# Sums within PSUM in a feed-forward layer: shared partial sums copied bank to bank, and seven products for the first output block

## The chip, the cores and the metric

The kernel runs on one core of a Trainium2 chip. The metric is the device time of one execution in microseconds (us); less is better. The engines are TensorE (PE in the profile; PEld is its loading of weights), VectorE (DVE), ScalarE (ACT), GpSimd (POOL) and SyncE (SP), which issues most transfers between HBM and the core's memory, SBUF. Matmuls write into PSUM: eight banks of 128 x 512 fp32.

## The reference

One transformer layer on 16 sequences of 256 rows with 512 values each: cross-attention with 16 heads, then a feed-forward part. All of it is fp32.

```python
x = x + xattn(layernorm(x), ctx, mask, mask, Wq, bq, Wk, bk, Wv, bv)
# feed-forward: the weights are given as indices into a table of 16 values
def ghost_linear(x, idx, lut):
    return einsum('bsh,oh->bso', x, lut[idx])
y = layernorm(x)
gate = ghost_linear(y, gate_idx, lut)      # 512 -> 1376
up   = ghost_linear(y, up_idx, lut)        # 512 -> 1376
h    = silu(gate) * up
x    = x + ghost_linear(h, down_idx, lut)  # 1376 -> 512
```

The 16 x 256 rows of attention's output are 32 tiles of 128 rows. In the kernel they are taken as 8 blocks (`nblocks`) of 512.

## The kernel before, in words

The instructions of every engine stand in the order in which the program writes them (`manual_schedule`); the framework adds the waits. Attention takes the first 980 us and is not touched by the change, except that its pool of two double PSUM banks, `ps_a`, stays open afterwards. A second pool, `ps_b`, has four single banks. While attention runs, VectorE also looks up the weights: the indices become table values through bit tests and predicated copies (`look_up`). What is not looked up by then is done in the feed-forward part.

**Gate and up.** The index tiles become the weights `wg`, `wu` (512 x 1376 each, in four slices of 128) and later `wd` (1376 x 512, in 11 slices, the last of 96 rows). `gate_up(n, 0)` (L920) takes the first 128 hidden values of blocks n = 0 to 3 in the plain way: 2 x 4 products into a double bank of `ps_a`, Silu on ScalarE, the product with `up` on VectorE. All the rest goes in *units* (`unit`, L937): a unit takes one column `o` of 128 hidden values and one pair `p` of two blocks, and computes gate and up for both, a 2 x 2 by 2 x 2 block product, with seven half-size products instead of eight (Winograd's form of Strassen). Operands that are sums or differences of weights are in `sw` and, in place, in `wu` (`combine_w`); those of activations are in `xe` and, in place, in the turned activations `xT` (`combine_x`). A unit's seven products each take one bank of `ps_b`: two slices, which the trace shows as four matmul instructions of 512 columns. Seven additions on VectorE (L951) join them, ScalarE copies the first product and does two Silus, GpSimd does two multiplications (L974, L980), and the results `ha` and `hb`, tiles of 128 x 512, are stored to HBM (`store_h`, `hds`). There are 42 units, in the order written in `order`.

Between the additions of a unit, `fill(ns)` (L909) issues VectorE work from a list, `todo`: the lookups that are left and the sums of weights. A budget `room` in estimated ns rations it. `hooks` are three places in each unit at which the rows of the blocks 4 to 7 are loaded, normalized and turned (`turn_blocks`; the transposes go to a bank of `ps_a`).

**Down.** After the units, `load_h(1)` and `load_h(2)` load two blocks of hidden values from HBM (block 0 was loaded during pair 3, into tiles that had become free). The tiles of the new pool `hp` take memory that the units' pools (`sw`, `ht`) held until `first.close()`. Then VectorE makes the operands `t2`, `t4` from `wd` and `combine_h(1)` those of block 1. Block 0 goes the plain way: `down(0)` (L1129) has four row tiles, each of 11 slices of `wd` into one bank, 88 matmul instructions of 512 columns, and one addition of the residual rows `x2t`, which `load_x2` fetches. Blocks 1 to 7 go through `down7(n, t)` (L1143), two calls a block, of seven products each (1, 2, 6, 7, 5, 4, 3 in this order, 256 columns wide, five slices each and one more for the 96 rows in 2, 5, 4 and 3), joined by ten additions on VectorE. The residual rows are loaded at the top of the call and enter with the second addition, `add(p1, p1, xrs[0][:, lo])`. Between the two calls `combine_h(n + 1)` prepares the next block, and after them `load_h(n + 2)` follows.

Of the kernel before, what the change touches and what calls it, by code (L numbers as in the profile page):

```python
# [9 lines left out]
F32 = mybir.dt.float32  # L10
# [9 lines left out]
def kernel(  # L20
# [62 lines left out]
    ps_a = ctx.enter_context(tc.tile_pool(name="ps_a", bufs=2, space=PSUM))  # L83
# [99 lines left out]
    x3pool = []  # L183
# [20 lines left out]
    def turn2(k):  # L204
        n, t = divmod(k, 4)
        if t == 0:
            pool = xpool if n % 4 < FIRST else x3pool[0]
            xTs[n] = pool.tile([P, NH, 4 * P], F32, tag="xT", name=f"xT_{n}")
        if n < FIRST:
            pt = ps_b.tile([P, 512], F32, tag="b", name=f"pt_{k}")  # L210
        else:
            pt = ps_a.tile([P, 2, 512], F32, tag="a", name=f"pt_{k}")[:, 0, :]
        xn = xns.pop(k)
        for h in range(NH):
            nc.tensor.transpose(pt[:, h * P : (h + 1) * P], xn[:, h * P : (h + 1) * P], ident)  # L215
        nc.scalar.copy(xTs[n][:, :, t * P : (t + 1) * P], pt.rearrange("p (h r) -> p h r", r=P))


    with ExitStack() as att:
        ac = att.enter_context(tc.tile_pool(name="att_const", bufs=1))  # L220
# [584 lines left out]
    with ExitStack() as ffn:  # L805
        wd_pool = ffn.enter_context(tc.tile_pool(name="wd", bufs=1))
        xep = ffn.enter_context(tc.tile_pool(name="xe", bufs=2))
        x3pool.append(ffn.enter_context(tc.tile_pool(name="xT3", bufs=1)))
        first = ffn.enter_context(ExitStack())
        sp = first.enter_context(tc.tile_pool(name="ffns", bufs=1))  # L810
        lp = first.enter_context(tc.tile_pool(name="lookup2", bufs=1))
# [51 lines left out]
        def lookups():  # L863

            left = list(pieces_left())
            ids = {}

            def load(j):
                if j < len(left):
                    rows, n = left[j][1].shape  # L870
                    ids[j] = lp.tile([P, T], I32, tag="idx", name=f"idx_l{j}", bufs=2)[:rows, :n]
                    nc.sync.dma_start(ids[j], left[j][1])

            def each():
                for j, (to, of) in enumerate(left):
                    rows, n = of.shape
                    ops = look_up(
                        lambda tag: lp.tile([P, T], I32, tag=tag, name=f"{tag}_l{j}")[:rows, :n],
                        to, ids.pop(j),
                    )  # L880
# [39 lines left out]
        def gate_up(n, o):  # L920
# [3 lines left out]
            ps = ps_a.tile([P, 2, 512], F32, tag="a", name=f"pgu_{n}_{o}")  # L924
            for i, w in enumerate((wg, wu)):
                for h in range(NH):
                    nc.tensor.matmul(  # L927
                        ps[:rows, i, :], w[:, h, at], xTs[n][:, h, :],
# [3 lines left out]
            nc.scalar.activation(sg[:rows], ps[:rows, 0, :], AF.Silu)  # L932
            ht = f1.tile([P, 4 * P], F32, tag="ht", name=f"ht_{n}_{o}")
            v.tensor_tensor(ht[:rows], sg[:rows], ps[:rows, 1, :], ALU.mult)
            store_h(n, o, ht, rows)

        def unit(p, o, hooks):  # L937

# [5 lines left out]
            def product(i, a, b):  # L944
                ps = ps_b.tile([P, 512], F32, tag="b", name=f"p{i}_{p}_{o}")[:rows]
                for h in range(2):
                    nc.tensor.matmul(ps, a[:, h, at], b[:, h, :], start=h == 0, stop=h == 1)  # L947
                return ps

            def add(to, ps, other):  # L950
                v.tensor_tensor(to, ps, other, ALU.add)  # L951

            p1 = rpool.tile([P, 4 * P], F32, tag="us1", name=f"p1_{p}_{o}", bufs=1)[:rows]
            nc.scalar.copy(p1, product(1, a11, b11))
            w = rpool.tile([P, 4 * P], F32, tag="us0", name=f"w_{p}_{o}", bufs=5)[:rows]
            add(w, product(6, sw[:, 1], xe[:, 1]), p1)
            hooks[0]()
            fill(1000)
            sg = rpool.tile([P, 4 * P], F32, tag="rb", name=f"sg_{p}_{o}", bufs=1)[:rows]
            add(sg, product(2, a12, b21), p1)  # L960
            nc.scalar.activation(sg, sg, AF.Silu)  # L961
            fill(1000)
            r = rpool.tile([P, 4 * P], F32, tag="us0", name=f"r_{p}_{o}", bufs=5)[:rows]
            add(r, product(7, a21, xe[:, 0]), w)
            hooks[1]()
            fill(1000)
            p5 = product(5, sw[:, 0], t1)
            add(w, p5, w)
            hb = f1.tile([P, 4 * P], F32, tag="ht", name=f"hb_{p}_{o}")[:rows]
            add(hb, p5, r)  # L970
            fill(350)
            ha = f1.tile([P, 4 * P], F32, tag="ht", name=f"ha_{p}_{o}")[:rows]
            add(ha, product(4, a22, xe[:, 2]), r)
            nc.gpsimd.tensor_tensor(ha, ha, sg, ALU.mult)  # L974
            store_h(2 * p, o, ha, rows)
            hooks[2]()
            fill(1000)
            add(w, product(3, sw[:, 2], b22), w)
# [3 lines left out]
            fill(2500)  # L982
# [69 lines left out]
        hs = {}  # L1052
        for i, (p, o) in enumerate(order):
            if p < 2 and o in (5, 8):
                while o not in ready:
                    next(todo)[1]()
            if (p, o) == (3, 2):

                parts = [xpool.tile([P, NH, 4 * P], F32, tag="xT", name=f"h0_{j}") for j in range(2)]
                parts.append(xep.tile([P, 3, 2, 4 * P], F32, tag="xe", name="h0_2")  # L1060
                             .rearrange("p a b t -> p (a b) t"))
                hs[0] = []
                for j, part in enumerate(parts):
                    for q in range(4 * j, min(4 * j + 4, NO)):
                        hs[0].append(part[:, q - 4 * j, :])
                for j, part in enumerate(parts[:2]):
                    nc.sync.dma_start(part, hds[0][4 * j : 4 * j + 4].rearrange("o p t -> p o t"))
                nc.sync.dma_start(parts[2][:, 0:2], hds[0][8:10].rearrange("o p t -> p o t"))
                rows = rows_of(NO - 1)
                nc.sync.dma_start(parts[2][:rows, 2, :], hds[0][NO - 1, :rows, :])  # L1070
            unit(p, o, [lambda i=i, j=j: run(hooks.pop((i, j), ())) for j in range(3)])
        for _, op in todo:
            op()
        first.close()
        hp = ffn.enter_context(tc.tile_pool(name="ffnh", bufs=2))

        def load_h(n):
            h = hp.tile([P, NO, 4 * P], F32, tag="h", name=f"h_{n}")
            rows = rows_of(NO - 1)
            nc.sync.dma_start(h[:, 0 : NO - 1, :], hds[n][0 : NO - 1].rearrange("o p t -> p o t"))  # L1080
            nc.sync.dma_start(h[:rows, NO - 1, :], hds[n][NO - 1, :rows, :])
            return h

# [6 lines left out]
        wl, wh, wz = wd[:, 0:HO], wd[:, HO : 2 * HO], wd[:last_rows, NO - 1]  # L1090

# [6 lines left out]
        hn = {1: load_h(1), 2: load_h(2)}  # L1098
        t2 = part_of(x3pool[0].tile([P, NH, 4 * P], F32, tag="xT", name="t2"), 0)
        t4 = hp.tile([P, HO, 2 * P], F32, tag="t4", name="t4", bufs=1)  # L1100
        s1s = [None, part_of(xpool.tile([P, NH, 4 * P], F32, tag="xT", name="s1_1"), 0)]
        se = [None, xep.tile([P, 3, 2, 4 * P], F32, tag="xe", name="se_1")]
        v.tensor_tensor(t2, wh[:, :, hi], wl[:, :, hi], ALU.subtract)
        v.tensor_tensor(t2, t2, wl[:, :, lo], ALU.add)
        v.tensor_tensor(t4, wh[:, :, lo], t2, ALU.subtract)

        def combine_h(n):

            h = hn[n]
            s1, e = s1s[n % 2], se[n % 2]  # L1110
            s2, s4 = part_of(e, 0), part_of(e, 1)
            d = e.rearrange("p a b t -> p (a b t)")[:last_rows, 2 * HO * 2 * P : (2 * HO + 1) * 2 * P]
            a11, a21 = h[:, 0:HO, lo], h[:, 0:HO, hi]
            a12, a22 = h[:, HO : 2 * HO, lo], h[:, HO : 2 * HO, hi]
            yield v.tensor_tensor(s1, a21, a22, ALU.add)
            yield v.tensor_tensor(s2, s1, a11, ALU.subtract)
            yield v.tensor_tensor(a21, a11, a21, ALU.subtract)
            yield v.tensor_tensor(s4, a12, s2, ALU.subtract)
            z = h[:last_rows, NO - 1]
            yield v.tensor_tensor(d, z[:, lo], z[:, hi], ALU.subtract)  # L1120
# [5 lines left out]
        def new_ob(i, name):  # L1126
            return rpool.tile([P, T], F32, tag=("rb", "xr")[i], name=name, bufs=1)

        def down(n):  # L1129
            xrs = [load_x2(4 * n + t) for t in range(4)]  # L1130
            for t in range(4):
                po = ps_b.tile([P, 512], F32, tag="b", name=f"po_{n}_{t}")
                for o in range(NO):
                    rows = rows_of(o)
                    nc.tensor.matmul(  # L1135
                        po, hs[n][o][:rows, t * P : (t + 1) * P], wd[:rows, o, :],
                        start=(o == 0), stop=(o == NO - 1),
                    )
                ob = new_ob(t % 2, f"ob_{n}_{t}")
                v.tensor_tensor(ob, po, xrs[t], ALU.add)  # L1140
                store_rows(4 * n + t, ob)

        def down7(n, t):  # L1143

            h = hn[n]
# [105 lines left out]
```

## Time and profile before

| | |
|---|---|
| time, median of 3 runs | 1805.18 us (1804.65 to 1806.34) |
| the profiled execution | 1806.96 us, its span 1805.2 us |
| busy share of the span | PE 99%, DVE 81%, ACT 44%, POOL 28% |
| attention | up to 980 us |
| four `gate_up` calls | 980 to 1011.7 us |
| 42 units | 1011.7 to 1525.4 us |
| `down(0)` | 1525.4 to 1563.2 us |
| 14 calls of `down7` | 1563.2 us to the end |

The profile is of one execution. Its tables give, for each engine, how long it was busy, what ended the idle time before its instructions (the releaser), and the chain of work that ended last, followed back from the last instruction. Line numbers (L947) are those of the kernel before. A group such as `p<-xe,wu` is named by the tiles that an instruction writes and reads. A transfer's row on SP's queue shows when SP issued it, not when it landed. The trace's ends of matmuls are modelled, so the distance between the starts of two products is the better measure of their cost.

### The profile page before, as it was taken

What the parts mean: (1) busy time and instruction counts of PE and PEld (TensorE: products, weight loads), DVE (VectorE), ACT (ScalarE), POOL (GpSimd) and SP (SyncE); (2) the same over time, 40 slices, a digit from 0 to 9 for tenths busy, and PEclk for the clock granted to TensorE, in tenths of its full rate; (3) what the DMA queues carried; (4) which work ended last, traced back from release to release, by engine and by line L of the source; (5) the groups of instructions that cost most, each with busy time, mean ns of one, the idle gap of its engine ahead of it and who ended that gap; (6) DMA issues with size and microseconds to landing.
All of it is one profiled execution on the core that took longest, in us unless ns stands there. A gap on an engine that the chain in (4) does not pass through costs nothing.

```text
span 1805.2 us, 28544 instructions
## 1 busy us (share of the span) xinstructions
PE 1785.9 (99%) x10914; PEld 822.4 (46%) x10914; DVE 1460.8 (81%) x2030; ACT 798.1 (44%) x1523; POOL 500.3 (28%) x467
## 2 busy tenths in 40 slices
PE   8999999999999999999999999999999999999999
PEld 4333333333333333333343444444444444688887
DVE  6898899999898999998987799998989995353352
ACT  1777777777777777777775111112121111000000
POOL 4334333434343433344332122221222222000000
PEclk9999999999999999999999999999999999999999
DMA  6445544333433344444433111222121311444441
GB/s 184 126 149 149 146 124 123 124 105 111 128 122 116 95 128 140 145 115 141 122 102 92 59 53 66 80 87 92 68 99 49 115 45 59 169 133 135 170 133 58
DMA packets 118824, 201.07 MB, mean 111 GB/s; under 512 B 21780, under 2 KB 23960, under 8 KB 118688
## 3 DMA queue, kind: packets, MB, share of 16 engines
q1 hardware_dynamic: 114416, 196.21, 34.2%
q0 software_dynamic: 3168, 1.86, 0.5%
q8 instruction: 86, 1.41, 0.3%
q10 hardware_dynamic: 1104, 1.19, 0.2%
q14 instruction: 50, 0.41, 0.1%
HBM read 135.83 MB, written 58.10 MB: 107 GB/s over the span
## 4 chain that ended last, share of the span: by engine, by line
PE 91%; DVE 4%; DMA 2%; ACT 1%; issue 0%; SPq 0%; POOL 0%; ACTq 0%; POOLq 0%; DVEq 0%
PE p L947 27%; PE pa L490 15%; PE pv L537 12%; PE pb L498 11%; PE q L1154 10%; PE pv L413 3%; PE pq L413 3%; PE pk L413 3%; PE po L1135 2%; DVE nm L506 1%; DMA x2t<-x 1%; PE q L1159 1%; PE pgu L927 1%; PE pt L215 1%; PE pv L516 1%; DVE chosen L161 0%
## 5 line engine op out<-in xcount | busy, mean ns | idle before, releaser
L506 DVE TENSOR_REDUCE nm<-pa 128x2 f32<-128x1024 f32 x512 | 602.3, 1218 | 84.4 <-PE pb L498 79.3
L510 ACT ACTIVATE pt<-pb 128x512 f32<-128x512 f32 x1024 | 530.4, 602 | 105.5 <-PE pb L498 104.2
L490 PE MATMUL pa<-kp,qp 32*128 32x512 f32 x2048 | 513.9, 616 | 7.3 <-DVE nm L506 3.8
L498 PE MATMUL pb<-qp,kp 32*128 32x512 f32 x2048 | 517.5, 617 | 0.0
L490 PEld LDWEIGHTS pa<-kp,qp 32*128 32x128 f32 x2048 | 177.0, 184 | 201.0 <-DVE nm L506 151.7
L537 PE MATMUL pv<-pt,va 128*32 128x512 f32 x2048 | 246.2, 598 | 0.0
L498 PEld LDWEIGHTS pb<-qp,kp 32*128 32x128 f32 x2048 | 209.6, 183 | 74.0 <-issue 42.0
L947 PE MATMUL p<-xe,wu 128*128 128x512 f32 (+1 forms) x336 | 158.0, 592 | 0.3 <-DVE w L951 0.3
L947 PE MATMUL p<-xT,sw 128*128 128x512 f32 (+1 forms) x336 | 157.9, 592 | 0.0
L947 PE MATMUL p<-xT,wg 128*128 128x512 f32 (+1 forms) x336 | 157.9, 592 | 0.0
L974 POOL TENSOR_TENSOR ha<-ha,sg 128x512 f32<-128x512 f32 (+1 forms) x42 | 61.1, 1456 | 343.2 <-DVE ha L951 332.7
L979 ACT ACTIVATE w<-w 128x512 f32<-128x512 f32 (+1 forms) x42 | 26.5, 630 | 250.6 <-DVE w L951 250.6
L537 PEld LDWEIGHTS pv<-pt,va 128*32 128x32 f32 x2048 | 53.4, 109 | 173.1 <-ACT pt L510 97.1
L521 POOL DMA_DIRECT2D qp<-mx x64 | 38.4, 601 | 310.9 <-DVE mx L520 290.5
L1170 ACT COPY q<-q 128x256 f32<-128x256 f32 x14 | 5.2, 373 | 255.1 <-PE q L1154 255.1
L542 ACT COPY us<-pv 128x512 f32<-128x512 f32 x128 | 75.0, 586 | 94.7 <-PE pv L537 94.7
L947 PEld LDWEIGHTS p<-xe,wu 128*128 128x128 f32 (+1 forms) x336 | 62.9, 187 | 81.9 <-issue 72.0
L947 PEld LDWEIGHTS p<-xT,wg 128*128 128x128 f32 (+1 forms) x336 | 62.6, 187 | 78.8 <-issue 75.6
L947 PEld LDWEIGHTS p<-xT,sw 128*128 128x128 f32 (+1 forms) x336 | 62.1, 187 | 75.9 <-issue 74.7
L961 ACT ACTIVATE sg<-sg 128x512 f32<-128x512 f32 (+1 forms) x42 | 26.5, 630 | 143.4 <-DVE sg L951 143.4
L549 POOL TENSOR_TENSOR us<-us,us 128x512 f32<-128x512 f32 x64 | 82.4, 1287 | 15.1 <-ACT us L542 15.0
L429 POOL TENSOR_TENSOR natk<-natk,mb 128x512 f32<-128x512 f32 x31 | 41.0, 1322 | 147.1 <-ACT natk L426 141.8
(208 smaller groups left out, 2385.5 us busy)
## 6 DMA issues: line engine op xcount, KB each, us to landing
x2t<-x SPq DMA_DIRECT2D x96, 256.0 KB
h<-h SPq DMA_DIRECT2D x7, 2560.0 KB
kp<-kd SPq DMA_DIRECT2D x62, 256.0 KB
qp<-qd SPq DMA_DIRECT2D x62, 256.0 KB
h<-ha SPq DMA_DIRECT2D x38, 256.0 KB
h<-hb SPq DMA_DIRECT2D x38, 256.0 KB
rb<-rd SPq DMA_DIRECT2D x32, 256.0 KB
xr<-in_x_dram SPq DMA_DIRECT2D x32, 256.0 KB
```

Source lines behind the costliest of these rows:

```text
L413: nc.tensor.matmul(ps[32 * j : 32 * j + 32], weights(o, slice(first + 32 * j, first + 32 * j + 32)), moving(o), start=(o == 0), stop=(o == ...
L429: nc.gpsimd.tensor_tensor(t, t, mb, ALU.mult)
L490: nc.tensor.matmul(pa[:, jj, :], qps[ua % 4][at, ca * P : (ca + 1) * P], kps[ua % 4][at, :], start=True, stop=True,)
L498: nc.tensor.matmul(pb, kps[ub % 4][at, cb * P : (cb + 1) * P], qps[ub % 4][at, :], start=True, stop=True,)
L506: nc.vector.tensor_reduce(nms[ua][:, 2 * half : 2 * half + 2, ca], pa, AX.X, ALU.max, negate=True)
L510: nc.scalar.activation(pts[sb][:, j, :], pb, AF.Exp)
L537: nc.tensor.matmul(ps[32 * j : 32 * j + 32, :], va[:, at : at + 32], pt[:, j, :], start=(i == 0), stop=(i == 1),)
L542: nc.scalar.copy(us[u, half], ps)
L549: nc.gpsimd.tensor_tensor(a, a, b, ALU.add)
L947: nc.tensor.matmul(ps, a[:, h, at], b[:, h, :], start=h == 0, stop=h == 1)
L974: nc.gpsimd.tensor_tensor(ha, ha, sg, ALU.mult)
L1154: nc.tensor.matmul(ps, a[:, o, first_t], b[:, o, :], start=o == 0, stop=o == HO - 1 and not more,)
```

## The change

It has three parts.

1. *Units.* PSUM is divided anew: `ps_a` closes with attention, and `ps_f` opens, with three banks `ae` and one bank `pt` for the transposes. In a unit the first product goes to a bank `pa`, and ScalarE copies it to a bank `pb` of `ps_b`. Product 6 is accumulated onto `pa`, which ScalarE copies to `pc`; product 7 is accumulated onto `pa` again, which is copied to `pd`. Product 2 goes onto `pb`, 3 onto `pc`, 4 onto `pd`: their matmuls add to what ScalarE put there. Product 5 (`pe`) is copied to SBUF (`p5`), and VectorE adds it to `pa` and to `pc`. The multiplication for `ha` moves from GpSimd to VectorE and is held until the next unit has issued its first product (`held`). The arguments of `fill` become larger.
2. *Lookups and gate/up of column 0.* The lookup tiles become parts of one tile, `look`, that stays until the end; `gate_up` takes two single banks of `ps_b`.
3. *Block 0.* It goes through `down7` too. Its operands are put into the memory of `wg` and `wu`. `before_down` gives the nine steps that VectorE needs for them; two are issued in the last unit, three before `down7(0, 0)`, and four inside it, one behind each of its first four additions. The blocks' hidden values are loaded in a low part (five slices) and a high part (six); the low part of block 1 is loaded into `look` at unit (3, 5), after the rest of `todo`.

```diff
-    ps_a = ctx.enter_context(tc.tile_pool(name="ps_a", bufs=2, space=PSUM))
...
     with ExitStack() as att:
+        ps_a = att.enter_context(tc.tile_pool(name="ps_a", bufs=2, space=PSUM))
...
+        ps_f = ffn.enter_context(tc.tile_pool(name="ps_f", bufs=3, space=PSUM))
...
         def unit(p, o, hooks):
...
+            def product(ps, a, b, onto=True):
+                for h in range(2):
+                    nc.tensor.matmul(
+                        ps, a[:, h, at], b[:, h, :], start=h == 0 and not onto, stop=h == 1,
+                        skip_group_check=onto,
+                    )
+
+            def copied(name, ps):
+                to = bank(name)
+                nc.scalar.copy(to, ps)
+                return to
+
+            pa = bank("pa", ps_f, "ae")
+            product(pa, a11, b11, onto=False)
+            pb = copied("pb", pa)
+            fill(600)
+            if held:
+                held.pop()()
+            pe = bank("pe", ps_f, "ae")
+            product(pe, sw[:, 0], t1, onto=False)
+            p5 = rpool.tile([P, 4 * P], F32, tag="us1", name=f"p5_{p}_{o}", bufs=1)[:rows]
+            nc.scalar.copy(p5, pe)
+            fill(2000)
+            product(pa, sw[:, 1], xe[:, 1])
+            pc = copied("pc", pa)
+            hooks[0]()
+            fill(2000)
+            product(pb, a12, b21)
+            sg = rpool.tile([P, 4 * P], F32, tag="rb", name=f"sg_{p}_{o}", bufs=1)[:rows]
+            nc.scalar.activation(sg, pb, AF.Silu)
+            fill(2000)
+            product(pa, a21, xe[:, 0])
+            pd = copied("pd", pa)
+            hooks[1]()
+            hb = f1.tile([P, 4 * P], F32, tag="ht", name=f"hb_{p}_{o}")[:rows]
+            v.tensor_tensor(hb, pa, p5, ALU.add)
+            fill(1000)
+            product(pc, sw[:, 2], b22)
             w = rpool.tile([P, 4 * P], F32, tag="us0", name=f"w_{p}_{o}", bufs=5)[:rows]
...
+            v.tensor_tensor(w, pc, p5, ALU.add)
             nc.scalar.activation(w, w, AF.Silu)
             nc.gpsimd.tensor_tensor(hb, hb, w, ALU.mult)
             store_h(2 * p + 1, o, hb, rows)
-            fill(2500)
+            product(pd, a22, xe[:, 2])
+            hooks[2]()
+            fill(1700)
+
+            def hold():
+                ha = f1.tile([P, 4 * P], F32, tag="ht", name=f"ha_{p}_{o}")[:rows]
+                v.tensor_tensor(ha, pd, sg, ALU.mult)
+                store_h(2 * p, o, ha, rows)
+
+            held.append(hold)
...
+        def before_down():
+
+            c = combine_h(0)
+            yield next(c)
+            yield next(c)
+            yield v.tensor_tensor(t2, wh[:, :, hi], wl[:, :, hi], ALU.subtract)
+            yield v.tensor_tensor(t2, t2, wl[:, :, lo], ALU.add)
+            yield next(c)
+            yield v.tensor_tensor(t3, wh[:, :, hi], wl[:, :, hi], ALU.subtract)
+            yield v.tensor_tensor(wl[:, :, hi], wl[:, :, hi], wl[:, :, lo], ALU.subtract)
+            yield v.tensor_tensor(t4, wh[:, :, lo], t2, ALU.subtract)
+            yield from c
...
+            if (p, o) == (3, 5):
+                for _, op in todo:
+                    op()
+                h_parts[1] = [(0, look[:, 0:HO])]
+                load_part(1, *h_parts[1][0])
+            if (p, o) == order[-1]:
+                pre = before_down()
+                hooks[i, 1].append(lambda: next(pre))
+                hooks[i, 2].append(lambda: next(pre))
             unit(p, o, [lambda i=i, j=j: run(hooks.pop((i, j), ())) for j in range(3)])
...
         def load_h(n):
...
+            low = look[:, 0:HO] if n % 2 else hp.tile([P, HO, 4 * P], F32, tag="hl", name=f"hl_{n}", bufs=1)
+            h_parts[n] = [(0, low)]
+            load_part(n, 0, low)
+            load_high(n)
...
+        def down7(n, t, pre=iter(())):
...
             xrs = [load_x2(4 * n + t), load_x2(4 * n + t + 2)]
...
             def add(to, ps, other):
                 v.tensor_tensor(to, ps, other, ALU.add)
+                next(pre, None)
...
-        for _ in combine_h(1):
-            pass
-        down(0)
...
+        load_high(1)
+        load_h(2)
+        for _ in range(3):
+            next(pre)
+        down7(0, 0, pre)
+        new_e(1)
+        for n in range(nblocks):
+            if n:
+                down7(n, 0)
             if n + 1 < nblocks:
                 for _ in combine_h(n + 1):
                     pass
             down7(n, 1)
```

## The prediction, made before the changed kernel was run

> **What bounds the kernel now.** I read the page first: part 1 for the busy shares, part 4 for the chain that ended last. Then I asked for TensorE's waits from 975 us on, where the changed code begins, and for the timelines of one unit and of the passage from the units to the down products.
>
> ```profile
> PE 1785.9 (99%) x10914; PEld 822.4 (46%) x10914; DVE 1460.8 (81%) x2030; ACT 798.1 (44%) x1523; POOL 500.3 (28%) x467
> PE 91%; DVE 4%; DMA 2%; ACT 1%; issue 0%; SPq 0%; POOL 0%; ACTq 0%; POOLq 0%; DVEq 0%
> ```
>
> TensorE (PE) is busy for 1785.9 of 1805.2 us and carries 91% of the chain. VectorE (DVE) at 81%, ScalarE (ACT) at 44% and GpSimd (POOL) at 28% only matter where they make PE wait. How often they do, in the stretch that the change touches:
>
> ```profile
> PE pt L215 <- ACT xT L216: 1.5, 2, 0.8
> PE q L1154 <- DVE ob L1166: 1.3, 2, 0.9
> PE p L947 <- DVE hb L951: 0.8, 1, 0.8
> PE pgu L927 <- POOL rb L592: 0.7, 1, 0.7
> PE p L947 <- DVE w L951: 0.3, 1, 0.3
> ```
>
> The columns are us in total, times, longest. The 42 units (L947) lose 0.8 + 0.3 = 1.1 us altogether, so relieving VectorE there can give back no more than that. What is left to gain is PE work itself. From the chain in order of time and the timeline:
>
> ```profile
> 1525.40 37.78 PE po L1135 x88
> 1563.18 4.32 PE q L1154 x20
> 1580.03 4.32 PE q L1154 x20
> ...
> 1501.20 1.88 PE L947 MATMUL p<-xT,wg 128*128 128x512 f32 x4
> 1502.92 1.88 PE L947 MATMUL p<-xe,sw 128*128 128x512 f32 x4
> 1503.17 0.59 ACT L954 COPY p<-p 128x512 f32<-128x512 f32 x1 [0.42 <-PE p L947]
> 1504.64 1.88 PE L947 MATMUL p<-xT,wg 128*128 128x512 f32 x4
> ```
>
> The first two columns are start and us. Down products of block 0 take 37.78 us in the plain form; one call of `down7` takes 1580.03 - 1563.18 = 16.85 us. In a unit the starts of successive products lie 1502.92 - 1501.20 = 1.72 us apart. The copy of a product starts 0.25 us after the product's last issue slot (1503.17 against 1502.92) and takes 0.59 us.
>
> **The change, part by part.** The sum is made against the profiled execution's span, 1805.2 us; that execution took 1806.96 us with what lies around the span, while the three timed runs have the median 1805.18. So differences in the span are added to 1805.18. A measurement of this kernel tells about 0.2%, 3.6 us, from no change.
>
> *Units.* Each keeps 7 products of 4 matmul instructions, 7 x 1.72 = 12.0 us of PE, times 42 as before: nothing there. VectorE loses four of seven additions of 0.68 us (42 x 4 x 0.68 = 114 us), GpSimd one of two multiplications of 1.47 us (about 61 us); ScalarE gains three copies of about 0.6 us (75 us), being busy 1.8 of 12 us in a unit now. None of this is on the path; its worth is at most the 1.1 us of waits. In exchange PE gets three new waits per unit: product 6 onto the sum that `pb` was copied from, 7 after the copy `pc`, 4 after the copy `pd`. Each time one other product (5, 2, 3) of 1.72 us lies between the product that is copied and the waiting one, and the copy needs 0.25 + 0.59 = 0.84 us of it, which leaves 0.88 us. No row shows ScalarE writing PSUM; its rows beside this, 0.373 us (128x256 copy) and 0.63 us (Silu), bound it, and I take 0.59: the cover holds up to 1.47 us. In front of these copies on ScalarE's queue stand the Silu of `w`, which waits for VectorE's addition, and the transposes' copies; with the units' VectorE order that addition may be about 2.9 us late before `pb` is, and one `combine_x` (4 x 1.23 us) fits into its idle time. I take back half of the 1.1 us: -0.6, with 0 to -1.1 for the range. The `fill` budgets rise from 6.85 to 9.3 us a unit, so the lookups, whose last instruction now ends at 1495.7, two and a half units before the end, are done near unit 30 of 42; the forced rest at (3, 5) finds nothing, and the load of block 1's low part that follows it has ten units to land. The store of `ha` moves into the next unit, on SP behind whatever hook 2 loads: nobody waits for it but the third `ht` buffer, a unit later, so 0.
>
> *Gate and up of column 0.* Two single banks for one double one; the four calls stay 32 + 16 + 16 instructions on PE. The banks they inherit from the scores were emptied by 980.05 (copy of the last `pv`), and the one needed then is used from 982.8. The 1.5 us of the transposes stay: one `pt` bank now, and the second transpose already waits for the first one's copy. 0.
>
> *Block 0 by seven products.* 37.78 us become 2 x 16.85 = 33.70: -4.08 us, if nothing waits. But the plain form needed nothing from VectorE. The new one needs `s1`, `s2`, `t2`, `t3`, the turned halves of `h` and `wl`, `t4`, `s4`, in VectorE instructions of 1.48 us (rows of L1103, L1115 to L1118 and L1195), nine steps, of which four come inside `down7`, each behind one of its additions. Call T0 the time of its first product (1525.2 now). Unhindered, product 6 starts at T0 + 4.75, product 7 at T0 + 6.9, product 5 at T0 + 9.1. On VectorE two steps run in the last unit, the held product of `ha` comes at T0 + 1.6 and three steps follow until about T0 + 6.2. The addition behind product 6 ends at T0 + 7.5, `t3` at T0 + 9.1: product 7 starts 2.2 us late.
>
> *The wait that I expect to decide.* The second addition in `down7`, `add(p1, p1, xrs[0])`, needs the residual rows `x2t`, and the step behind it in VectorE's order is the subtraction in `wl`, which product 5 reads. The loads of `x2t` are issued at the top of `down7(0, 0)`, behind `load_high(1)` and `load_h(2)` on SP's queue. Now they also stand behind two blocks, and this is when they land:
>
> ```profile
> 1528.68 0.32 SPq L824 DMA_DIRECT2D h<-hb  x1
> 1531.07 0.38 SPq L1080 DMA_DIRECT2D h<-h  x1
> 1539.26 3.11 SPq L187 DMA_DIRECT2D x2t<-x  x4
> ...
> 1541.41 1.49 DVE L1115 TENSOR_TENSOR s<-h 128x1280 f32<-128x1280 f32 x1 [9.05 <-DMA h<-h]
> 1550.49 1.34 DVE L1140 TENSOR_TENSOR ob<-po,x2t 128x512 f32<-128x512 f32 x2 [2.92 <-DMA x2t<-x]
> ...
> 1599.07 1.31 SPq L187 DMA_DIRECT2D x2t<-x  x2
> 1610.64 0.43 DVE L1166 TENSOR_TENSOR q<-q,x2t 128x256 f32<-128x256 f32 x1 [6.33 <-DMA x2t<-x]
> ```
>
> The first block load waits 2.1 us for the last store of the units to land (1528.68 to 1531.07, less its issue), since it takes over their memory. Block 1 (2560 + 192 KB, 2.82 MB) is there 10.34 us after that, and both blocks with one `x2t` (5.90 MB) after 19.42 us. That cost nothing, because the plain products filled four banks and PE had 37.78 us. In the changed kernel the low part of block 1 is loaded early, so ahead of the first `x2t` lie 1.51 + 2.82 = 4.33 MB, with itself 4.59 MB: between the two points, 10.34 + (4.59 - 2.82) / (5.90 - 2.82) x 9.08 = 15.6 us. The last stores are issued at about T0 + 2.0 (`ha` ends at T0 + 2.3 at worst, `hb` on GpSimd at T0 + 1.4 to 1.9), so the load starts near T0 + 4.2 and `x2t` is there at T0 + 19.8. The addition (0.43) and the subtraction (1.49) follow, with 0.2 us to PE: product 5 starts at T0 + 21.9 instead of T0 + 9.1, a stall of 12.8 us that contains the 2.2 of product 7. After it `t4` and `s4` come in time: three products of 2.59 us end at T0 + 29.7. The second call's `x2t` finds the queue empty, as the second calls of the later blocks do now.
>
> The sum: -0.6 - 4.1 + 12.8 = +8.1, that is 1805.18 + 8.1 = 1813.3 us. Bounds of the stall: with no wait for the stores 1.8 us less, at the best rate of single us in the trace (some 0.39 MB per us) 1.3 us less; at the rate of the later case (3.08 MB in 12.8 us from 1597.81 to 1610.6, with two stores still under way) 19.1 instead of 15.6 us, 3.5 more. With the units' bounds the likeliest case holds 1810 to 1818.
>
> A rule that speaks against a stall of this length: before, PE's longest pause is 2.50 us, before 1.14 us of `pa` products at 17.77 that are as fast as those at 24.27, with the granted clock at 1.00. [...]
>
> [...]
>
> **The rivals.** *The loads are hidden (no stall by x2t).* If `x2t` is there by T0 + 9, what remains is `t3`: -4.1 - 0.6 + 2.2 = -2.5, 1802.7 us, no change by the measure. For it: all loads use one set of engines, and small ones might pass; against it: 1599.07 to 1610.64 above, a load of 256 KB that waited behind one block. *All steps are hidden, t3 too:* -4.7, 1800.5, faster. It asks VectorE to be 2.2 us ahead of its own order, so it is unlikely. *ScalarE becomes the units' bound:* if a copy within PSUM, with what queues before it, takes over 1.47 us, PE loses the excess three times a unit, 126 us per us of it; at 0.03 us over, 3.8 us on top of the forecast. For it: three copies in a chain, on a queue that also holds Silu; against it: all rows are within 0.63 us and ScalarE is busy 31% of a unit afterwards. [...]
>
> **How the numbers follow.** The forecast has 0.77, the hidden loads 0.11, all hidden 0.07, ScalarE 0.05 (slower, about 1817 or more). So faster 0.07, same 0.11, slower 0.82. The range 1802.5 to 1818.5 takes in the forecast with its bounds and the hidden loads; outside lie the fast case, most of ScalarE's and the forecast's tails.
>
> **What would show it.** Right: the waits list `DVE q <- DMA x2t` of some 10 us and `PE q <- DVE wd` of some 10 to 13 us once, both 10 to 22 us after the first down product; the units at 12.0 us each without PE waits, lookups gone near unit 30; later blocks as before. Wrong: PE without a pause over 3 us between the units and block 1, or products in units more than 1.72 us apart behind `pb`, `pc` or `pd`.

## The result, and the profile after

The changed kernel takes 1817.88 us (median of 4 runs, 1816.28 to 1818.82); the kernel before, measured again beside it, 1805.76 us (4 runs, 1804.65 to 1810.88). The ratio is 1.0061 (95% interval 1.004 to 1.0081): 12 us slower, where 8 had been forecast. The profiled execution of the changed kernel took 1816.28 us, its span 1814.5 us at a mean granted clock of 0.996.

The page first, part 1 (busy us, share of the span, instructions):

```profile
PE 1783.5 (98%) x10982; PEld 836.5 (46%) x10982; DVE 1340.0 (74%) x1886; ACT 870.8 (48%) x1651; POOL 435.8 (24%) x425
```

The work moved as the diff says: VectorE is busy 121 us less, GpSimd 64 us less, ScalarE 73 us more. PE's own work is 2.4 us less, not 4.1, and its span has grown by 9.3 us. So it waits, and the list of TensorE's waits from 975 us on (us in total, times, longest) says for what:

```profile
PE q L1199 <- DVE wd L1106: 9.9, 1, 9.9
PE pa L956 <- ACT pb L963: 2.1, 1, 2.1
PE q L1199 <- DVE wu L1105: 2.0, 1, 2.0
PE pt L214 <- ACT xT L215: 1.4, 2, 0.7
PE pgu L930 <- issue: 0.7, 1, 0.7
PE q L1199 <- DVE ob_rb L1211: 0.5, 2, 0.3
PE q L1199 <- DVE wg L1103: 0.4, 1, 0.4
```

Three of these seven stand at block 0's first call of `down7` (`wg` holds `t2`, `wu` holds `t3`, `wd` the low half that product 5 reads), one in the units. Block 0 in the timelines of SP, VectorE and TensorE; the first column is the start, the second the us, and the brackets hold the idle time before and what ended it (here and below, selected rows):

```profile
1527.81 0.32 SPq L828 DMA_DIRECT2D h<-ha  x1
1530.23 0.38 SPq L1087 DMA_DIRECT2D hh<-h  x1
1534.23 1.62 SPq L186 DMA_DIRECT2D x2t<-x  x2
...
1533.63 1.48 DVE L1105 TENSOR_TENSOR wu<-wd 128x1280 f32<-128x1280 f32 x1
1545.48 0.42 DVE L1211 TENSOR_TENSOR q<-q,x2t 128x256 f32<-128x256 f32 x1 [10.37 <-DMA x2t<-x]
1545.83 1.48 DVE L1106 TENSOR_TENSOR wd<-wd 128x1280 f32<-128x1280 f32 x1
...
1525.47 4.48 PE L1199 MATMUL q<-wd,h 128*128 128x256 f32 x20
1535.17 2.43 PE L1199 MATMUL q<-wu,h 128*128 128x256 f32 x10 [1.98 <-DVE wu L1105]
1547.46 3.83 PE L1199 MATMUL q<-wd,wg 128*128 128x256 f32 x10 [9.86 <-DVE wd L1106]
1551.56 2.32 PE L1199 MATMUL q<-wu,h 128*128 128x256 f32 x10
```

T0, the first down product, is at 1525.47. The residual rows `x2t` are issued at 1534.23, behind the block loads that begin at 1530.23, and are there at 1545.48; the subtraction into `wd` is done at 1547.31, and product 5 starts at 1547.46 = T0 + 21.99. It then takes 3.83 us for ten instructions where the next product takes 2.32. The reason is in the windows (length; busy us of PE, PEld, DVE, ACT, POOL; granted clock; DMA share; GB/s):

```profile
1537.00:1547.00 10.00, 0.59 (x3) 0.19 (x1) 1.51 (x2) 0.00 (x0) 0.00 (x0) 0.66 0.87 309
1547.40:1549.40 2.00, 1.94 (x5) 1.61 (x6) 2.00 (x4) 0.00 (x0) 0.00 (x0) 0.50 0.00 0
```

In the pause the queues move 309 GB/s, and the granted clock falls; product 5 starts at 0.50. Narrower windows place the change to half clock at 1540.1 and its end at 1550.4: 10.24 us, which begin in the pause and end in the work behind it.

And the wait in the units, once in 42, in the unit whose hook also holds the `combine_x` of a turned pair of row blocks:

```profile
1250.97 1.23 DVE L853 TENSOR_TENSOR xe<-xT 128x1024 f32<-128x1024 f32 x1 [3.51 <-ACT xT L215]
1254.75 1.23 DVE L856 TENSOR_TENSOR xe<-xT,xe 128x1024 f32<-128x1024 f32 x1
1255.89 0.69 DVE L99 BATCH_NORM_STATS2 bn_f<-x2t 128x6 f32<-128x512 f32 x1
1257.29 0.68 DVE L993 TENSOR_TENSOR w<-pc,p 96x512 f32<-96x512 f32 x1
1258.06 0.63 ACT L994 ACTIVATE w<-w 96x512 f32<-96x512 f32 x1 [7.12 <-DVE w L993]
1258.60 0.57 ACT L963 COPY pb<-pa 128x512 f32<-128x512 f32 x1
1259.22 2.83 PE L956 MATMUL pa<-xe,sw 128*128 128x512 f32 x4 [2.09 <-ACT pb L963]
1261.84 2.78 PE L956 MATMUL pb<-xT,wg 128*128 128x512 f32 x4
```

VectorE does four steps of `combine_x` and a statistics instruction, and only then the additions of the unit before; ScalarE waits 7.12 us with the Silu of `w`, and the copy `pb` that TensorE needs stands behind that Silu on the same engine. The products after this pause take 2.8 us instead of the 1.88 of the others: 3.41 us at half clock here too (1260.23 to 1263.64, granted clock 0.50).

To compare kernels, I cut each profiled execution at four landmarks: the first gate and up product, T0, block 1's first product, the end of the span. (Where the feed-forward part begins differs between the ten profiled executions by up to 5 us, in attention, which no kernel here changes.)

| kernel | first gate/up to T0 | block 0 | from block 1 on |
|---|---|---|---|
| before | 545.97 | 37.78 | 242.18 |
| after | 547.84 (+1.9) | 48.12 (+10.3) | 240.91 (-1.3) |

This one execution began 1.6 us earlier than that of before; 1.9 + 10.3 - 1.3 - 1.6 = 9.3, the difference of the spans.

### The profile page after: what moved, and what is told of

It is laid out like the page before. It is cut to its first block, busy times and chain, and to the rows that moved or that the text cites. A ratio compares the mean times of both kernels' runs of the same rounds, so it can differ in the third digit from the quotient of the medians.

```text
span 1814.5 us, 28718 instructions
## 1 busy us (share of the span) xinstructions
PE 1783.5 (98%) x10982; PEld 836.5 (46%) x10982; DVE 1340.0 (74%) x1886; ACT 870.8 (48%) x1651; POOL 435.8 (24%) x425
## 4 chain that ended last, share of the span: by engine, by line
PE 91%; DVE 3%; DMA 2%; ACT 1%; SPq 0%; issue 0%; DVEq 0%; ACTq 0%
PE pa L490 15%; PE pv L537 12%; PE pa L956 12%; PE q L1199 12%; PE pb L498 11%; PE pb L956 4%; PE pd L956 4%; PE pc L956 4%; PE pe L956 4%; PE pv L413 3%; PE pq L413 3%; PE pk L413 3%; DMA x2t<-x 2%; PE pgu L930 2%; DVE nm L506 1%; PE q L1204 1%
## 5 line engine op out<-in xcount | busy, mean ns | idle before, releaser
L995 POOL TENSOR_TENSOR hb<-hb,w 128x512 f32<-128x512 f32 (+1 forms) x42 | 57.2, 1362 | 465.4 <-ACT w L994 448.2
L989 DVE TENSOR_TENSOR hb<-pa,p 128x512 f32<-128x512 f32 (+1 forms) x42 | 29.0, 689 | 148.3 <-ACT pd L963 148.3
L956 PE MATMUL pa<-xe,sw 128*128 128x512 f32 (+1 forms) x168 | 79.9, 598 | 2.1 <-ACT pb L963 2.1
L956 PE MATMUL pb<-xT,wg 128*128 128x512 f32 (+1 forms) x168 | 79.9, 598 | 0.0
L956 PE MATMUL pc<-xT,sw 128*128 128x512 f32 (+1 forms) x168 | 79.0, 592 | 0.0
L956 PE MATMUL pa<-xT,wg 128*128 128x512 f32 (+1 forms) x168 | 78.9, 592 | 0.0
L956 PE MATMUL pd<-xe,wu 128*128 128x512 f32 (+1 forms) x168 | 78.9, 592 | 0.0
L956 PE MATMUL pa<-xe,wu 128*128 128x512 f32 (+1 forms) x168 | 78.9, 592 | 0.0
L956 PE MATMUL pe<-xT,sw 128*128 128x512 f32 (+1 forms) x168 | 78.9, 592 | 0.0
```

The costliest lines, as they stand in the source:

```text
L956: nc.tensor.matmul(ps, a[:, h, at], b[:, h, :], start=h == 0 and not onto, stop=h == 1, skip_group_check=onto,)
L995: nc.gpsimd.tensor_tensor(hb, hb, w, ALU.mult)
```

## The experiments

The theory: block 0 loses its time because the `x2t` of its first call wait on SP's queue behind two blocks' loads (e1, e8, e3, e4), the units lose a little because `combine_x` delays an addition that ScalarE must have before its copy (e2, e5), and product 5 is slow because the clock was halved in the pause (e7). The rival of the first: the block would be as late for its steps or loads anyway. The first four kernels ran together (before: 1806.21 us, 23 runs), the other four too (before: 1805.57 us, 23 runs).

**Residual rows first.**

```diff
-def down7(n, t, pre=iter(())):
+def down7(n, t, pre=iter(()), xrs=None):
-    xrs = [load_x2(4 * n + t), load_x2(4 * n + t + 2)]
+    xrs = xrs or [load_x2(4 * n + t), load_x2(4 * n + t + 2)]
...
+xr0 = [load_x2(0), load_x2(2)]
 load_high(1)
 load_h(2)
...
-down7(0, 0, pre)
+down7(0, 0, pre, xr0)
```

> The residual rows x2t of block 0's first call are loaded ahead of the blocks 1 and 2, not behind them; nothing else differs from the changed kernel. Theory (the residual rows queue behind 4.33 MB, and VectorE's subtraction for product 5 stands behind the addition that needs them): the pause of 9.9 us before product 5 is gone, the one of 2.0 us before product 7 (t3) stays, TensorE's clock stays at full there (product 5 in 2.6 us, not 4.1), so 9.9 + 1.5 = 11.4 us less than the changed kernel, about 1806.5 us beside 1805.5 of the kernel before. Rival (VectorE's own order is the wait: the nine steps take as long wherever the rows are): product 5 still starts 20 us after the first product, about 1818 us.

1806.35 us, ratio 0.9997 (0.9989 to 1.0006). TensorE's waits now begin so, and `wd` is not among them:

```profile
PE pa L956 <- ACT pb L963: 2.1, 1, 2.1
PE q L1199 <- DVE wu L1105: 2.0, 1, 2.0
```

Block 0 takes 36.59 us, 11.5 less than after, because two loads of 256 KB are issued earlier. Nothing else in block 0 is different, so the loss there was this wait and what followed from it.

**Residual rows between the two blocks.** As e1, with the `xr0` line between `load_high(1)` and `load_h(2)`.

> The residual rows of block 0's first call are loaded behind the high part of block 1 (1.51 MB) and ahead of block 2 (2.82 MB). Theory (a first-come queue of bytes): they land 2.82 MB x 2.95 us per MB = 8.3 us earlier than in the changed kernel, 6.9 us after the first block load is issued, so 11.7 us after the first down product; product 5 starts 13.7 us after it instead of 22.0, and block 0 takes about 38.4 us, 1.8 more than with the rows first. Rival (all transfers under way share the engines, so what is issued behind delays the rows as much): product 5 still starts some 20 us after the first product.

1809.01 us, ratio 1.0019 (1.0008 to 1.0029). SP's queue, VectorE and the wait of TensorE:

```profile
1530.12 0.38 SPq L1087 DMA_DIRECT2D hh<-h  x1
1531.11 1.12 SPq L186 DMA_DIRECT2D x2t<-x  x2
1532.28 0.45 SPq L1087 DMA_DIRECT2D hl<-h  x1
...
1537.70 0.43 DVE L1211 TENSOR_TENSOR q<-q,x2t 128x256 f32<-128x256 f32 x1 [2.72 <-DMA x2t<-x]
...
PE q L1199 <- DVE wd L1106: 2.2, 1, 2.2
```

The rows land 7.58 us after the first block load is issued (1530.12 to 1537.70), against 15.25 after (1530.23 to 1545.48). Ahead of them are 1.51 MB instead of 4.33. In those 7.58 us the queue moved 2.10 MB, of which 2.03 are the loads up to and with the two of `x2t` (1.51 + 0.52), so next to nothing of the 2.82 MB behind them had moved: the queue served its loads nearly in order, and the rival falls. Block 0 takes 40.73 us, 2.3 more than expected, of which 1.8 are a product 5 of 4.35 instead of 2.59 us: this short pause, too, came with half clock, for 3.41 us, which the expectation had left out.

**The combination one hook earlier.**

```diff
-turn_blocks(4, 3 * order.index((1, 8)) - 1)
+turn_blocks(4, 3 * order.index((1, 8)) - 2)
```

> The turning of blocks 4 and 5 is moved one hook ahead, so that the four subtractions of combine_x for pair 2 come at hook 0 of unit (1, 10) and not at hook 1, right ahead of the two additions. Theory (the additions come 7 us late, the Silu of w behind them on ScalarE holds up the copy pb, TensorE pauses 2.1 us and then runs at half clock for 3.4 us): both are gone, 2.1 + 1.9 = 4.0 us less than the changed kernel, about 1813.9 us; the pause before product 5 of the down products is as before. Rival (the pause belongs to the copy within PSUM itself or to the unit's transposes): the pause moves along with the hook and the time stays at about 1818 us.

1814.22 us, ratio 1.0045 (1.0033 to 1.0057). Of the waits, `pa <- ACT pb` is gone, and the rest stays:

```profile
PE q L1199 <- DVE wd L1106: 9.9, 1, 9.9
PE q L1199 <- DVE wu L1105: 2.0, 1, 2.0
```

In the unit, the combination now starts at 1248.60 instead of 1250.97. The addition still stands behind it on VectorE, but comes 2.4 us earlier too, and ScalarE has its copy done (at 1257.03) before TensorE needs it (1257.98):

```profile
1254.92 0.68 DVE L993 TENSOR_TENSOR w<-pc,p 96x512 f32<-96x512 f32 x1
1255.70 0.63 ACT L994 ACTIVATE w<-w 96x512 f32<-96x512 f32 x1 [3.82 <-DVE w L993]
1256.46 0.57 ACT L963 COPY pb<-pa 128x512 f32<-128x512 f32 x1
1257.98 1.88 PE L956 MATMUL pa<-xe,sw 128*128 128x512 f32 x4
```

The stretch up to T0 takes 543.79 us: 4.05 less than after, 2.2 less than before. So the new order of a unit is worth 2.2 us, and one hook too late turns that into +1.9. In this trace no two successive instructions of TensorE in the units start more than 0.43 us apart.

**New units, block 0 in the plain form.** Block 0's `down(0)` of before put back (88 instructions, four banks of `po`), with `combine_h(1)` and the steps `t3` and `wl` where before had them; the early load of the low half stays.

> The changed units alone: block 0's down products are plain again (88 matmul instructions of 512 columns), the block loads and everything else as in the changed kernel. Theory: the units cost the 4.0 us of the one pause and its half clock, less the 1.1 us of waits that they had before: 1805.5 + 2.9 = 1808.4 us, and the half clock shows once. Rival 1 (the units are free, the whole change in time lies at block 0): 1805.5 us. Rival 2 (the three waits for copies cost a little in every unit): units over 12.02 us apart, and more than 1810 us.

1805.74 us, ratio 1.0001 (0.9992 to 1.0009), 2.7 us under the expectation, nearer to the rival's number. Block 0 takes 37.78 us, as before. The 2.1 us pause is there, and in the profiled execution without half clock:

```profile
PE pa L956 <- ACT pb L963: 2.1, 1, 2.1
```

Up to T0 it takes 546.14 us, 1.7 less than after (3.41 / 2 = 1.7), and the later blocks 241.16 us, 1.0 less than before, of which I had expected nothing. My expectation carried the clock loss as a certainty and missed the gain in the later blocks.

**Old units, block 0 by seven products.** `unit()` as before (additions on VectorE, both stores inside the unit, nothing held), and the load of block 1's low part moves to the last unit.

```diff
-pb = copied("pb", pa)
...
-held.append(hold)
+add(w, product(6, sw[:, 1], xe[:, 1]), p1)
...
+add(ha, product(4, a22, xe[:, 2]), r)
+nc.gpsimd.tensor_tensor(ha, ha, sg, ALU.mult)
+store_h(2 * p, o, ha, rows)
...
-if (p, o) == (3, 5):
+if (p, o) == order[-1]:
```

> Block 0 by seven products alone: the units are those of the kernel before (additions on VectorE, one copy, the budgets of before), the rest of the lookups is forced before the last unit. Theory: +12.9 of pauses +1.5 of half clock -4.1 of products: 1805.5 + 10.3 = 1815.8 us, one half-clock stretch and not two. Rival (the pause at block 0 is caused by the units' new order on VectorE and GpSimd): product 5 starts sooner by several us, under 1812 us.

1820.32 us, ratio 1.0074 (1.0062 to 1.0086): 14.1 us slower than before, 3.8 more than expected. The wait, the last store of the units, the first block load, and the arrival of `x2t`:

```profile
PE q L1177 <- DVE wd L1085: 11.5, 1, 11.5
...
1532.53 0.32 SPq L828 DMA_DIRECT2D h<-hb  x1
1534.88 0.38 SPq L1066 DMA_DIRECT2D hh<-h  x1
...
1550.27 0.43 DVE L1189 TENSOR_TENSOR q<-q,x2t 128x256 f32<-128x256 f32 x1 [12.00 <-DMA x2t<-x]
```

The old unit makes `hb` last, and its store goes out at 1532.53 = T0 + 4.9, where after's last store, of `ha`, goes at T0 + 2.3. The loads wait for it, so all is some 2.5 us later; from the first load to the addition it is again 15.39 us. Half clock lasts 13.65 us here, and block 0 takes 52.07 us. (This execution has 3.41 us more of it at 18.5 us, in attention.) So the loss belongs to block 0's part of the change alone; the new units make it smaller, since they free the block's memory earlier. What I had missed is that the start of the loads is itself set by the unit's last store.

**Both repairs (e1 and e2).**

> Both edits at once: residual rows of the first call ahead of the block loads, and combine_x of pair 2 one hook earlier. Theory (the two pauses are the whole loss and are independent): from the first gate-up product to the first down product 543.8 us as in the run with the earlier combine_x, block 0 36.6 us as in the run with the rows first, the rest 241.0 us: 821.4 us where the kernel before has 825.9, so 4.5 us less than the kernel before. Rival (what is won in the units comes back as a later start of something at the passage): block 0 over 38 us.

1803.46 us, ratio 0.9993 (0.9983 to 1.0002). Its profiled execution has 543.80 us to T0 and 36.59 us in block 0, as the two repairs predict, and a span 4.4 us shorter than before's; the medians differ by 2.1 only. The eleven runs reach from 1800.1 to 1807.7: those at 1803.5 or less have a mean granted clock of 0.999 to 1.0, those at 1805.7 or more 0.997 to 0.998. The profile is of one of the former; which stretches lose the clock in the latter no trace here shows.

**The best order that the runs point to.** e5, and `t3` as the first of the nine steps, so that it is done in the last unit; and each later block's first residual rows loaded ahead of the block after next.

```diff
 c = combine_h(0)
+yield v.tensor_tensor(t3, wh[:, :, hi], wl[:, :, hi], ALU.subtract)
 yield next(c)
 yield next(c)
...
-yield v.tensor_tensor(t3, wh[:, :, hi], wl[:, :, hi], ALU.subtract)
...
+hooks[i, 0].append(lambda: next(pre))
+hooks[i, 0].append(lambda: next(pre))
 hooks[i, 1].append(lambda: next(pre))
-hooks[i, 2].append(lambda: next(pre))
...
-    down7(n, 0)
+    down7(n, 0, xrs=ahead)
...
+    ahead = [load_x2(4 * n + 4), load_x2(4 * n + 6)]
     load_h(n + 2)
```

So three steps run in the last unit, one ahead of the held product, two before `down7(0, 0)` and three inside it. The edits came together; which of them gave how much is read from the waits alone.

> As with both edits, and besides the subtraction for t3 is the first of the nine steps, s1 and t3 run at hook 0 of the last unit, one more step each at hook 1, ahead of the held product and before the call; the residual rows of the first call of each later block are loaded ahead of the next block load. Theory (t3 in VectorE's order costs product 7 its 2.0 us and product 6 waits 0.4 for t2; the later pauses on the output additions are the same queue of loads): 2.4 + 0.7 = 3.1 us less than with both edits, 7.6 us less than the kernel before, a ratio of about 0.9958. Rival (product 7 waits for VectorE's total work, not for the order): block 0 stays at 36.6 us.

1797.63 us, ratio 0.9963 (0.995 to 0.9975): faster than both kernels, 7.9 us under before. The whole list of TensorE's waits from 975 us on:

```profile
PE pt L214 <- ACT xT L215: 1.4, 2, 0.7
PE pgu L930 <- issue: 0.7, 1, 0.7
```

No wait is left in the down products. By landmarks it has 543.80 us to T0 (-2.2), 33.85 us in block 0 (-3.9) and 239.9 us after it (-2.3).

**TensorE kept busy in the pause.** Eleven products of the identity, 22 instructions into the free `pt` bank, between product 7 and product 5 of block 0's first call; they add work and compute nothing that is used.

```diff
+if n == 0 and t == 0:
+    idle = ps_f.tile([P, 512], F32, tag="pt", name="idle", bufs=1)
+    for _ in range(11):
+        nc.tensor.matmul(idle, ident, wg[:, 0, 0:512], start=True, stop=True)
```

> The changed kernel with eleven products of the identity (22 matmul instructions, 9.4 us, into a bank that nobody reads) issued between product 7 and product 5 of block 0's first call: TensorE works through most of the 9.9 us pause. Theory (the slow product 5, 4.1 us instead of 2.6, is the halved clock after the pause): the pause stays in place, product 5 starts at the same distance from the first product, about 22 us, but takes 2.6 us, and there is no half-clock stretch: 1.5 to 2.4 us less than the changed kernel. Rival (product 5 is slow because the transfers or VectorE's steps use the same memory): product 5 as slow as before, or slower.

1815.52 us, ratio 1.0058 (1.0046 to 1.007). The timeline of TensorE:

```profile
1535.12 3.41 PE L1199 MATMUL q<-wu,h 128*128 128x256 f32 x10 [1.98 <-DVE wu L1105]
1538.32 10.36 PE L1228 MATMUL idle<-wg,ident 128*128 128x512 f32 x22
1548.52 2.32 PE L1199 MATMUL q<-wd,wg 128*128 128x256 f32 x10
```

Product 5 runs at its full rate, 2.32 us for the ten instructions that took 3.83, at a granted clock of 1.00. Its loads and VectorE steps are the same, so the slow product 5 was the clock and not its operands or the memory. Two things the expectation missed: the fillers end late, so that product 5 starts at T0 + 23.10, 1.1 us later than after, and there is a half-clock stretch, of 3.41 us, behind the 2.0 us pause before product 7 (3.41 us instead of 2.43), where after had none. So block 0 takes 47.73 us, only 0.4 less than after.

## Why the prediction was right or wrong, by its own steps

*The decisive wait* was right in place, cause and size. `x2t` was there 15.25 us after the first load (forecast 15.6), the load started at T0 + 4.76 (forecast T0 + 4.2), product 5 at T0 + 21.99 (forecast T0 + 21.9). Against the 9.15 us of e6, where nothing waits, that is 12.84 us late; the forecast said 12.8, the wait for `t3` included (1.98 measured, 2.2 forecast). That the sum fits to 0.1 us is in part luck: the loads started 0.6 later and were 0.35 shorter than forecast, and a wait of product 6 for `t2` (0.38) was not foreseen. e1 takes the position in the queue away: product 5 starts at T0 + 11.96, so 10.0 of the 12.84 us were the queue and 2.8 VectorE's order, and with the clock 11.5 us go. e8 puts the loads in the middle and gets a time in between.

*Block 0's products* were right: 33.85 us in e6 where 33.70 was forecast, -3.9 against -4.08.

*The clock* is the term that was left out of the sum. I put it aside because a 2.50 us pause in the trace of before had cost nothing (granted clock 1.00 from 14 to 20 us). Measured in block 0: product 5 with its last slice took 4.10 instead of 2.59 us, so 1.5 us; in e2 4.95 us, so 2.4. The longest pause in the trace of before was 2.5 us and could say nothing of one of 10 us; I let it decide. It did not even speak for its own length: in e4 the pause at the same place, of 2.31 us, is followed by half clock. With this term block 0 closes: 33.85 + 12.84 + 1.51 = 48.20 us, against 48.12 measured.

*The units* were mis-sized, and the forecast's own sign of being wrong, a product late behind `pb`, came true in one unit. The forecast of -0.6 is in the runs three numbers: -2.2 us with the combination placed earlier (e2), +0.2 with its 2.1 us pause (e1, e3), +1.9 with that pause and half clock after it (after). The ceiling of 1.1 us for what relief could give back was too low: the list of waits counts from modelled ends and leaves out the smallest, while from start to start the three pauses in before's units (at 1181, 1257 and 1361 us) cost 2.0 us. I had seen the ingredients, one `combine_x` in VectorE's idle time and the Silu of `w` ahead of the copies on ScalarE, and looked at them singly. The combination starts only when the transposed rows are there (1250.97), so VectorE's idle time before it was no cover; a statistics instruction followed it, and the Silu carried the delay to ScalarE's queue: 7.12 us of waiting there, of which TensorE's cover took all but 2.09. The copies themselves take 0.57 us (forecast 0.59), so the rival in which ScalarE bounds the units fell: no product waits for `pc` or `pd`. The lookups end at 1369.9 us; with the units' start at 1009.7 and 12.1 us each that is unit 29.8, as forecast.

*The later blocks* were forecast unchanged and are 1.3 us shorter. From start to start, before loses 2.3 us there in four pauses ahead of products that follow the slices of 96 rows (the list of waits shows two of them, for an output addition), after 1.0 us in two, and e6 nothing; 2.3 - 1.0 is the 1.3.

In sum, with forecasts in brackets: 1.9 in the units (-0.6), 10.3 in block 0 (8.7), -1.3 after it (0), together 10.9 (8.1). The medians give 12.1 us with an interval of 7 to 15, which holds 10.9. Of the rivals, the hidden loads and the hidden `t3` are refuted for this order of loads, and become real once the order is changed (e1, e6).

*When a pause brings half clock* can be read from the ten traces, though no run moved a pause on purpose. Every change of the granted clock that a trace records lies a whole multiple of 3.413 us behind the first record of that trace, at 4 to 7 us (after: 4.12, then 1260.23, 1263.64, 1540.12 and 1550.36, that is 368, 369, 450 and 453 steps). So each of the ten executions has its own grid of steps, and in them a pause counted by what fell into one step. Steps of after and e1 around the pause in the units, then of e4 and before around the pause in attention (PE's busy time comes second, the granted clock behind the fifth engine):

```profile
1256.82:1260.23 3.41, 1.32 (x4) 0.53 (x4) 3.38 (x5) 1.63 (x3) 1.41 (x1) 1.00 0.00 0
1260.23:1263.64 3.41, 3.41 (x6) 1.35 (x5) 2.02 (x4) 0.57 (x1) 0.06 (x1) 0.50 0.68 202
...
1255.23:1258.64 3.41, 1.80 (x5) 0.50 (x3) 3.38 (x7) 0.69 (x2) 0.00 (x0) 1.00 0.00 0
1258.64:1262.05 3.41, 2.93 (x7) 1.44 (x8) 3.34 (x5) 1.51 (x3) 1.47 (x1) 1.00 0.29 84
...
15.07:18.49 3.42, 1.11 (x10) 0.31 (x8) 2.03 (x5) 0.00 (x0) 0.00 (x0) 1.00 0.95 280
18.49:21.90 3.41, 3.41 (x24) 0.59 (x16) 2.55 (x4) 0.00 (x0) 0.00 (x0) 0.50 1.04 376
...
13.76:17.18 3.42, 1.51 (x5) 0.52 (x3) 0.87 (x2) 0.00 (x0) 0.00 (x0) 1.00 0.83 194
17.18:20.59 3.41, 2.82 (x24) 0.73 (x24) 2.80 (x6) 0.00 (x0) 0.00 (x0) 1.00 1.03 368
```

In after the pause lies in one step, which is idle for 3.41 - 1.32 = 2.09 us, and half clock follows; in e1 the border cuts it into 1.61 and 0.48, and nothing follows (e3: 0.78 and 1.30). Before's 2.50 us in attention are cut into 1.9 and 0.6, e4's 2.31 are not. Up to the end of the kernels, all nine changes from full to half clock follow a step in which TensorE was idle for 1.98 us or more, and no step at full clock with more than 1.99 us is without one.

What stays open: what decides at just 2.0 us, where one step of 1.98 us (e7) brought half clock and one of 1.99 (e5) did not, and whether a pause moved on purpose obeys the grid; that run was not made.

## What to carry to other kernels

When an operation gets its first use of a small load, look at what is in front of that load on its queue and not at its size: here two loads of 256 KB behind 4.33 MB cost 11.5 us, the slow work behind the pause included, and issuing them earlier gave all of that back. When work goes to another engine, follow what already stands on that engine's queue ahead of it, and who feeds that; here the new copy took 0.57 us, and ScalarE had waited 7.12 us ahead of it. And price a pause of TensorE at its length plus the slow work that can stand behind it: here 9.9 us and then 1.5 (after) or 2.4 us (e2), and 2.09 us with 1.7 behind it in after and none in e1.

## What the runs showed of the hardware

- One queue served its loads nearly in order: the same 256 KB were there 15.25 us after the first load's issue with 4.33 MB ahead of them, and 7.58 us after it with 1.51 MB ahead and the rest behind (e8), of which next to nothing had moved by then.
- In these ten traces the granted clock changed on a grid of 3.413 us whose place differed from execution to execution (a border at 1260.23 us in after, at 1258.64 in e1), and half clock lasted multiples of it: 3.41 us after a pause of about 2 us (2.09 in after), 10.24 in and after one of 9.9 us (after), 13.65 around one of 11.5 us (e4). It followed 1.98 to 2.31 us of idle time inside one step in six cases; 1.99 us in one step of e5 were not followed by it.
- Matmuls that add to what ScalarE copied into a PSUM bank, of which the trace of before has none, kept the pace of the others: in e2's 42 units, with three such products each, the instructions of 512 columns started 0.43 us apart throughout.
- A ScalarE copy from one PSUM bank to another took 0.57 us for 128x512 fp32 (0.56 for 96x512), where the copy from PSUM to SBUF in the same units took 0.585 (after).
